# Opening each gate graph with the product S1 T1, and issuing the sums for the next graph one beat sooner

## The chip, the cores and the metric

The kernel runs on one core of one Trainium2 chip. The metric is the time of one execution on the device, in microseconds (us). Beside it stands a profiled execution, whose trace gives the start and the length of every instruction on each engine: TensorE (PE, with its weight loads listed apart as PEld), VectorE (DVE), ScalarE (ACT), GpSimd (POOL), and the DMA queue that SyncE issues (SP).

## The reference, cut to what matters

There are 64 graphs with 256 nodes and 256 features each. Layer 0 is a graph convolution; its result is x2, and h2 is x2 after a layer norm and a relu. Layer 1 works on h2. A convolution with 17 taps along the nodes gives x_conv, message passing gives x_nmp, and a gated unit mixes them:

```python
x_in = jnp.concatenate([x_conv, x_nmp], axis=-1)
gi = x_in @ w_ih.T + b_ih
gh = x @ w_hh.T + b_hh              # x is h2 here
r = jax.nn.sigmoid(gi_r + gh_r)
z = jax.nn.sigmoid(gi_z + gh_z)
nn_ = jnp.tanh(gi_n + r * gh_n)
return (1.0 - z) * nn_ + z * x      # and then x2 is added
```

All numbers are 32-bit floats.

## The kernel before, in words

**Two stages.** The first stage, up to about 885 us, computes layer 0, the messages and the first part of the convolution, and starts the spectral convolution of graphs 0 to 15. The second stage computes the gates. It has four parts of 16 graphs. Part q computes the gates of 16 graphs and, in the first three parts, the spectral convolution of the next 16: first their spectra, then 24 products by frequency (`product`), three ahead of the gates and six inside each graph until they are used up, which is in the fourth graph. The inverse transform of these products runs on VectorE and GpSimd through the rest of the part. At its end `turn_outputs` transposes the outputs into the tile `xcT`, which the next part reads.

**One graph of gates** is `gates(ld, between, nxt)`. The r and z gates for two halves of 128 nodes would need four sums of six 128-row products. They are computed as seven (Strassen's scheme): each call of `three` is three accumulated matmuls, each of which has two records in the trace. Its inputs are plain tiles (`hx` from memory, `xcT`), sums of them called S1 to S4, and sums of weights called T1 to T4. The order on TensorE, with a name that the text uses for each:

- P1 into `ta` columns RC, P2 into `tb` RC, P3 into `tb` ZC, P5 = S1 T1 into `tc` ZC;
- `between[0]()`, a convolution product where there is one;
- P6 = S2 T2 onto `ta`, P7 = S4 W2 onto `tc`, the six matmuls of the n gate for the first half (`gates_n(ld, 0)`), P4 = S3 T3 onto `ta`;
- the rest of `between`, and `gates_n(ld, 1)`.

P1 and P5 accumulate onto a bias that ScalarE has copied into the bank ahead (`bank_of`). For the next graph the copy into `tc` is made in `first_rows`, behind the tanh of the first half, and the copy into `ta` in `second_rows`, one beat later. `tb` is claimed anew by each graph.

**Beats.** After each group of matmuls stands a `beat(us)`. `after(k, go)` puts off a piece of work for another engine to the (k+1)-th beat from there. A beat issues what has come due, in the order of registration, and then a share of the paced work of the inverse transform (`Paced`), as far as the room that the beat adds allows: a two-operand VectorE operation costs 0.5 for 256 elements and 0.85 for 512. All engines keep the program's order, so the place of an issue is the place in its engine's queue.

**The sums.** `gate_parts` returns two functions: `s12` (three VectorE operations: two adds that make S1, one subtraction that makes S2) and `s34` (three GpSimd operations that make S4 and S3). S1 and S2 have two buffers each, S3 and S4 one. For the first graph of a part they are called directly; for the others `gates` of the graph before registers them as `nxt`. A beat is counted here from the graph's start in a graph without products: beat 1 follows P1, and beats 7, 8 and 9 follow the n matmuls of the first half, P4, and the n matmuls of the second half.

Of the kernel before, what the change touches and what calls it, by code (L numbers as in the profile page):

```python
# [82 lines left out]
def add(e, o, a, b):  # L83
    e.tensor_tensor(o, a, b, ALU.add)
# [101 lines left out]
def gnn_kernel(  # L186
# [60 lines left out]
    def after(beats, go):  # L247
        due.append([beats, go])

    def come_due():  # L250
        now = []
        for d in list(due):
            d[0] -= 1
            if d[0] < 0:
                now.append(d[1])
                due.remove(d)
        for go in now:
            go()
# [286 lines left out]
    with ExitStack() as one:  # L545
# [11 lines left out]
        def beat(us):  # L557
            come_due()
            paced.issue(*(k * us for k in share))
# [93 lines left out]
        def taps_part(hold, oc, cc, k0):  # L653
            n = min(4, KW - k0)
            t = bank(f"t_w2_{oc}_{cc}_{k0}")
            for k in range(n):
                pe.transpose(
                    t[:, k * P : (k + 1) * P],
                    hold[oc][:, cc * P : (cc + 1) * P, k0 + k],
                    ident,  # L660
                )

            def keep():
                evict(
                    w2T[cc][:, k0 : k0 + n, oc * P : (oc + 1) * P],
                    t[:, : n * P].rearrange("p (k o) -> p k o", k=n),
                )
                if oc == DC - 1:
                    nc.sync.dma_start(
                        wt_d[k0 : k0 + n, cc * P : (cc + 1) * P].rearrange("k c o -> c k o"),  # L670
                        w2T[cc][:, k0 : k0 + n],
                    )
            after(0, keep)
            beat(0.4)
# [77 lines left out]
        def gate_turn(tag, dst, o0, i):  # L752
# [8 lines left out]
        parts = [  # L761
            [lambda oc=oc, cc=cc, k0=k0: taps_part(hold, oc, cc, k0)
             for cc in range(DC) for k0 in range(0, KW, 4)]
            for oc in range(DC)
        ]
# [532 lines left out]
    def outputs_turned(q):  # L1298
# [16 lines left out]
    RC, ZC = slice(0, D), slice(D, 2 * D)  # L1315
    W1 = [whT[:, 0], whT[:, 1], wiT[:, DC]]
    W2 = [wiT[:, 0], wiT[:, 1], wiT[:, DC + 1]]
    T1, T2, T3, T4 = (
        big.tile([P, 3, D], FP, tag=f"T{k}", name=f"T{k}") for k in range(1, 5)
    )  # L1320
# [17 lines left out]
    def gate_rows(ld):  # L1338
        n, q, g = ld["n"], ld["q"], ld["g"]
        ld["h2"] = h2 = io2.tile([P, NB, D], FP, tag="h2l", name=f"h2l_{n}")  # L1340
        nc.sync.dma_start(
            h2, h2_d[q][g * N : (g + 1) * N].rearrange("(c p) d -> p c d", p=P)
        )
        ld["x2"] = x2 = io2.tile([P, NB, D], FP, tag="x2l", name=f"x2l_{n}")
        nc.sync.dma_start(x2, x2_d[n].rearrange("(c p) d -> p c d", p=P))
# [31 lines left out]
    def three(dst, A, W, start):  # L1377
        for k in range(3):
            pe.matmul(
                dst, A[k], W[k], start=(start and k == 0), stop=(k == 2), skip_group_check=True  # L1380
            )

    def parts(S):
        return [S[:, k] for k in range(3)]

    def copied(ld, src, tag):
        ld[tag] = t = sm2.tile([P, D], FP, tag=tag, name=f"{tag}_{ld['n']}", bufs=1)
        act.copy(t, src)
# [3 lines left out]
    def bank_of(tag):  # L1392

        k = banks.get(tag, 0)
        banks[tag] = k + 1
        t = ps_gate.tile([P, 2 * D], FP, tag=tag, name=f"{tag}_{k}", bufs=1 + (tag == "n"))
        if tag == "n":
            act.copy(t, bnB)
        elif tag == "ta":
            act.copy(t[:, RC], brzB[:, RC])  # L1400
        else:
            act.copy(t[:, ZC], brzB[:, ZC])
        return t
# [3 lines left out]
    def gates_n(ld, nb):  # L1407

        pn = ready.pop(("n", nb))
        for off, pairs in (  # L1410
            (D, list(zip(ld["A1"][nb][:DC], (whT[:, c] for c in range(DC))))),
            (0, [(ld["A1"][nb][DC], wiT[:, DC])]
             + list(zip(ld["A2"][nb], (wiT[:, 0], wiT[:, 1], wiT[:, DC + 1])))),
        ):
            for k, (a, w) in enumerate(pairs):
                pe.matmul(
                    pn[:, off : off + D], a, w[:, 2 * D :],
                    start=False, stop=(k == len(pairs) - 1), skip_group_check=True,
                )
        ld[f"pn{nb}"] = pn  # L1420

    def gates_out(ld, nb):

        n, h2, x2, pn, rz = ld["n"], ld["h2"], ld["x2"], ld[f"pn{nb}"], ld["rz"][nb]
        uu = sm2.tile([P, D], FP, tag="u", name=f"u_{n}_{nb}")
        nn = sm2.tile([P, D], FP, tag="nn", name=f"nn_{n}_{nb}")
        df, ot = h2[:, nb, :], x2[:, nb, :]


        def inner():  # L1430
            vec.scalar_tensor_tensor(uu, rz[:, RC], 1.0, pn[:, D:], ALU.add, ALU.mult)
            vec.scalar_tensor_tensor(uu, uu, 0.5, pn[:, 0:D], ALU.mult, ALU.add)

        def outer():
            act.activation(nn, uu, AF.Tanh)
            ready["n", nb] = bank_of("n")


        def plain():
            e = vec if n == B - 1 and nb == NB - 1 else pool  # L1440
            e.tensor_tensor(df, df, nn, ALU.subtract)
            e.tensor_tensor(ot, ot, nn, ALU.add)

        def scaled():
            vec.scalar_tensor_tensor(df, rz[:, ZC], 1.0, df, ALU.add, ALU.mult)
            vec.scalar_tensor_tensor(ot, df, 0.5, ot, ALU.mult, ALU.add)
            dst = out[n].rearrange("(c p) d -> p c d", p=P)
            if n == B - 1:
                nc.sync.dma_start(dst[:, nb], ot)
            elif nb == NB - 1:  # L1450
                nc.sync.dma_start(dst, x2)

        after(2, inner)
        after(3, outer)
        after(4, plain)
        after(5 if n == B - 1 else 6, scaled)

    def gates(ld, between, nxt):


        n = ld["n"]
        ta, tc_ = ready.pop("ta"), ready.pop("tc")
        tb = ps_gate.tile([P, 2 * D], FP, tag="tb", name=f"tb_{n}", bufs=1)
        rz = [
            sm2.tile([P, 2 * D], FP, tag=f"rz{k}", name=f"rz_{n}_{k}", bufs=1) for k in range(NB)
        ]
        ld["rz"] = rz
        three(ta[:, RC], ld["A1"][0], [w[:, RC] for w in W1], False)
        after(1, lambda: copied(ld, ta[:, RC], "p1"))
        beat(1.3)  # L1470
        three(tb[:, RC], ld["A2"][0], [w[:, RC] for w in W2], True)
        after(2, lambda: add(vec, rz[0][:, RC], ld["p1"], tb[:, RC]))
        beat(1.3)
        three(tb[:, ZC], ld["A2"][1], parts(T4), True)
        beat(1.3)
        three(tc_[:, ZC], parts(ld["S1"]), parts(T1), False)
        after(1, lambda: copied(ld, tc_[:, ZC], "p5"))
        beat(1.3)
        between[0]()
        three(ta[:, RC], parts(ld["S2"]), parts(T2), False)  # L1480
        after(1, lambda: copied(ld, ta[:, RC], "u2"))
        beat(1.3)
        three(tc_[:, ZC], parts(ld["S4"]), [w[:, ZC] for w in W2], False)

        def first_rows():
            act.activation(rz[0], rz[0], AF.Tanh, scale=0.5)
            ready["tc"] = bank_of("tc")
        after(1, lambda: add(vec, rz[0][:, ZC], ld["u2"], tc_[:, ZC]))
        after(2, first_rows)
        beat(1.3)  # L1490
        gate_rows(ld)
        gates_n(ld, 0)
        gates_out(ld, 0)
        beat(2.6, v=0.2)
        three(ta[:, RC], parts(ld["S3"]), parts(T3), False)

        def second_rows():
            copied(ld, ta[:, RC], "u3")
            ready["ta"] = bank_of("ta")
            add(vec, rz[1][:, RC], ld["u3"], tb[:, ZC])  # L1500
        after(1, second_rows)
        after(2, lambda: add(pool, rz[1][:, ZC], ld["u3"], ld["p5"]))
        after(3, lambda: act.activation(rz[1], rz[1], AF.Tanh, scale=0.5))
        beat(1.3, v=0.4)
        for go in between[1:]:
            go()
        gates_n(ld, 1)
        gates_out(ld, 1)
        if nxt is not None:
            after(0, nxt[0])  # L1510
            after(1, nxt[1])
        beat(2.6, v=0.8, g=0.7)


# [10 lines left out]
    for q in range(1, GROUPS + 1):  # L1525
        share[:] = 0.6, 0.6, 0.3
        ld = gate_inputs(q - 1, 0)
# [19 lines left out]
        for g in range(NG):  # L1547
            share[:] = (0.42, 0.55, 0.3) if todo else (0.51, 0.62, 0.3)
            between = [todo.pop(0) if todo else lambda: None for _ in range(PER)]
            ahead, nxt = None, None  # L1550
            if g + 1 < NG:
                ahead = gate_inputs(q - 1, g + 1)
                nxt = gate_parts(ahead, xcT)
            gates(ld, between, nxt)
            ld = ahead
# [36 lines left out]
```

## Time and profile before

| what | value |
|---|---|
| median of 3 runs (lowest, highest) | 2079.03 us (2078.04, 2083.53) |
| profiled execution, its own time | 2078.45 us |
| its span, first to last instruction | 2076.7 us |
| TensorE busy | 2028.5 us, 98% of the span |
| its weight loads busy | 1727.0 us, 83% |
| VectorE busy | 1404.7 us, 68% |
| ScalarE busy | 997.5 us, 48% |
| GpSimd busy | 1108.9 us, 53% |
| mean granted TensorE clock | 0.997 |

A row of the profile gives the engine, the operation, the tiles that it writes and reads (written<-read), their shapes, and behind a bar the busy time and the mean of one; "idle before" is the time in which the engine had nothing to run ahead of it, with the engine and tile whose end released it. Since a helper records all operations, they carry the same line number, L102; the tiles tell them apart. In the timeline `rz<-u,tc` is VectorE's sum for the first half's z gate, `S<-hx,xcT` and `S<-hx` are the two adds of S1, `S<-S,hx` makes S2, `Xf` and `scr` are the inverse transform, `y` the banks of the convolution products.

### The profile page before, as it was taken

To read this page: it belongs to the slowest core of one execution; us is meant where nothing else is said; L and a number is where in the kernel's file an instruction comes from. 1 tells how busy PE (TensorE), PEld (TensorE's weight loads), DVE (VectorE), ACT (ScalarE), POOL (GpSimd) and SP (SyncE) were. 2 spreads that over 40 slices of the span, in tenths; PEclk is the share of its full clock that TensorE was granted. 3 is DMA by queue.
4 is the path that set the end of the run, shared out by engine and by line. 5 is a ranking of instruction groups with operands and counts; after the bars stand their busy time and mean duration, and the time that the engine had idled before them with its cause. 6 is when DMAs were issued, how large, how long until landed. Compare 5 with 4: busy or idle time off the path is not lost. (4 is left out here: it accounts for less than half of the span.)

```text
span 2076.7 us, 31189 instructions
## 1 busy us (share of the span) xinstructions
PE 2028.5 (98%) x9977; PEld 1727.0 (83%) x9977; DVE 1404.7 (68%) x3181; ACT 997.5 (48%) x2165; POOL 1108.9 (53%) x1313
## 2 busy tenths in 40 slices
PE   7999999999999999899999999999999999999998
PEld 6877777888888787788888888888888888888887
DVE  6656666544688887337889815989924989965444
ACT  5756666665457676522344532234442234443333
POOL 4343333334775665347667527766726767644433
PEclk9999999999999999999999999999999999999999
DMA  9697987657765554656333455533346424322231
GB/s 307 241 255 245 264 252 251 208 178 228 242 203 195 178 178 148 202 178 203 122 117 117 138 177 187 167 102 117 126 154 195 155 92 127 117 87 89 95 97 61
DMA packets 292456, 352.84 MB, mean 170 GB/s; under 512 B 19491, under 2 KB 232118, under 8 KB 291638
## 3 DMA queue, kind: packets, MB, share of 16 engines
q1 hardware_dynamic: 291680, 346.26, 52.5%
q0 software_dynamic: 288, 4.46, 0.6%
q8 instruction: 80, 1.31, 0.3%
q14 instruction: 82, 0.67, 0.1%
q10 hardware_dynamic: 326, 0.14, 0.0%
HBM read 224.43 MB, written 126.35 MB: 169 GB/s over the span
## 5 line engine op out<-in xcount | busy, mean ns | idle before, releaser
L102 DVE SCALAR_TENSOR_TENSOR Xf<-Xf 128x256 f32<-128x256 f32 (+1 forms) x248 | 185.7, 763 | 6.1 <-ACT Xf L102 5.1
L102 DVE TENSOR_TENSOR Xf<-y,k 128x256 f32<-128x256 f32 x184 | 69.0, 416 | 178.3 <-PE y L102 175.3
L102 PE MATMUL ta<-T,S 128*128 128x256 f32 x768 | 186.6, 379 | 0.0
L102 PE MATMUL y<-wf,Xf 128*128 128x256 f32 x768 | 182.4, 380 | 2.5 <-DVE Xf L102 1.4
L102 POOL TENSOR_TENSOR rz<-u,p 128x256 f32<-128x256 f32 x64 | 48.0, 749 | 244.6 <-ACT u L102 244.6
L102 POOL TENSOR_TENSOR rs<-ve,mhalf 128x2 f32<-128x2 f32 (+1 forms) x65 | 52.2, 803 | 226.8 <-DVE nm L102 221.6
L102 ACT ACTIVATE rz<-rz 128x512 f32<-128x512 f32 x128 | 80.2, 627 | 180.6 <-DVE rz L102 180.6
L102 PEld LDWEIGHTS y<-wf,Xf 128*128 128x128 f32 x768 | 144.0, 190 | 24.9 <-DVE Xf L102 2.6
L102 PEld LDWEIGHTS ta<-T,S 128*128 128x128 f32 x768 | 145.9, 190 | 19.8
L102 PE MATMUL n<-wiT,hx 128*128 128x256 f32 x512 | 152.3, 379 | 0.0
L102 POOL TENSOR_TENSOR xs<-Xf 128x256 f32<-128x256 f32 x92 | 69.9, 766 | 133.9 <-PE y L102 72.7
L102 DVE SCALAR_TENSOR_TENSOR h2l<-rz,h2l 128x256 f32<-128x256 f32 x128 | 102.8, 803 | 53.6 <-POOL h2l L102 53.6
L102 POOL TENSOR_TENSOR aT<-e,adjT 128x512 f32<-128x512 f32 x64 | 85.8, 1358 | 94.1 <-ACT e L102 94.1
L102 PE MATMUL n<-whT,hx 128*128 128x256 f32 x512 | 131.4, 379 | 0.0
L102 PE MATMUL n<-wiT,xcT 128*128 128x256 f32 x512 | 131.4, 379 | 0.0
L102 PE MATMUL o<-w0T,aggT 128*128 128x256 f32 x512 | 125.6, 388 | 5.7 <-ACT aggT L102 4.1
L102 PE MATMUL ag<-adjH,hs 128*128 128x256 f32 x512 | 123.0, 382 | 7.5 <-POOL adjH L102 6.1
L102 PE MATMUL nm<-aT,mso 128*128 128x256 f32 x512 | 123.0, 384 | 7.1 <-POOL aT L102 4.5
L102 PE MATMUL ms<-wmT,h2T 128*128 128x259 f32 x512 | 124.3, 385 | 1.5 <-DVE h2T L102 1.5
L102 POOL TENSOR_TENSOR adjH<-adjT,eye 128x512 f32<-128x512 f32 x64 | 83.6, 1306 | 76.8 <-ACT adjT L102 76.8
L102 PE MATMUL c<-w1T,h2T 128*128 128x256 f32 x512 | 122.8, 383 | 0.0
L102 PEld LDWEIGHTS o<-w0T,aggT 128*128 128x128 f32 x512 | 95.3, 191 | 28.7 <-issue 5.6
(183 smaller groups left out, 5253.1 us busy)
## 6 DMA issues: line engine op xcount, KB each, us to landing
wf<-wfd SPq DMA_DIRECT2D x284, 256.0 KB
wfd<-fo SPq DMA_DIRECT2D x32, 576.0 KB
x2d<-x SPq DMA_DIRECT2D x64, 256.0 KB
h2d<-h SPq DMA_DIRECT2D x64, 256.0 KB
hTd<-h2T SPq DMA_DIRECT2D x64, 256.0 KB
h1d<-c1o SPq DMA_DIRECT2D x64, 256.0 KB
xnd<-xnT SPq DMA_DIRECT2D x64, 256.0 KB
h1l<-h1d SPq DMA_DIRECT2D x64, 256.0 KB
```

The source lines that it names most:

```text
L102: return self.tc.keep_in_program_order(getattr(self.engine, op)(*args, **kwargs))
```

## The change

The call of `three` for P5, with the put-off copy of its result (`p5`) and a beat, moves from the fourth place to the first. P1, P2 and P3 follow it, one place later each. The registration of `nxt` moves from after `gates_n(ld, 1)` to ahead of the beat that follows P4, and the second of its functions is registered for two beats after its first possible one, not one.

```diff
         ld["rz"] = rz
+        three(tc_[:, ZC], parts(ld["S1"]), parts(T1), False)
+        after(1, lambda: copied(ld, tc_[:, ZC], "p5"))
+        beat(1.3)
         three(ta[:, RC], ld["A1"][0], [w[:, RC] for w in W1], False)
         after(1, lambda: copied(ld, ta[:, RC], "p1"))
         beat(1.3)
...
         three(tb[:, ZC], ld["A2"][1], parts(T4), True)
-        beat(1.3)
-        three(tc_[:, ZC], parts(ld["S1"]), parts(T1), False)
-        after(1, lambda: copied(ld, tc_[:, ZC], "p5"))
         beat(1.3)
         between[0]()
...
         after(3, lambda: act.activation(rz[1], rz[1], AF.Tanh, scale=0.5))
+        if nxt is not None:
+            after(0, nxt[0])
+            after(2, nxt[1])
         beat(1.3, v=0.4)
         for go in between[1:]:
             go()
         gates_n(ld, 1)
         gates_out(ld, 1)
-        if nxt is not None:
-            after(0, nxt[0])
-            after(1, nxt[1])
         beat(2.6, v=0.8, g=0.7)
```

So `s12` is issued at beat 8 in place of beat 9. In a graph without products `s34` is issued at beat 1 of the next graph as before; in a graph with products, where up to ten more beats lie between P4 and `gates_n(ld, 1)`, both come that much earlier.

## The prediction

> **What bounds the kernel now.** I read the page first, then the waits of TensorE in the gate stage, then the windows of three graphs, then timelines where a wait ended. The page:
>
> ```profile
> span 2076.7 us, 31189 instructions
> PE 2028.5 (98%) x9977; PEld 1727.0 (83%) x9977; DVE 1404.7 (68%) x3181; ACT 997.5 (48%) x2165; POOL 1108.9 (53%) x1313
> ```
>
> TensorE is busy all the time. A busy PE can still be stretched, so I took start to start: in the gates it is 216 ns per record wherever no wait shows. A graph without products has 66 records, 14.26 us, and the third of the windows below lasts 14.25. There is nothing to win in such a graph; the change can only take away, or make, waits of TensorE. Those from 885 us on, longest first, as total, times and longest:
>
> ```profile
> PE ta L102 <- ACT ta L102: 3.3, 3, 1.1
> PE yt L102 <- ACT xcT L102: 1.8, 6, 0.3
> PE y L102 <- DVE Xf L102: 1.4, 3, 0.5
> ```
>
> Three graphs as windows (starting at 1058.81, 1130.40 and 1942.07):
>
> ```profile
> 1058.81:1073.31 14.50, 14.41 (x67) 12.35 (x65) 12.08 (x23) 4.92 (x13) 10.55 (x12) 1.00 0.36 113
> 1130.40:1145.91 15.51, 14.41 (x68) 12.35 (x66) 14.42 (x23) 4.87 (x13) 12.83 (x14) 1.00 0.36 115
> 1942.07:1956.32 14.25, 14.25 (x68) 12.54 (x67) 6.92 (x14) 5.00 (x12) 5.92 (x8) 1.00 0.27 93
> ```
>
> The columns are length, then busy time of PE, PEld, DVE, ACT, POOL. Only the first line of waits is what the change aims at: P1 waiting for the bias in `ta`. Start to start it is 0.26 us more than 216 ns at the start of graph 9 (1073 us), 1.27 at graph 14 (1145 us), and 0.10 more on the next record each time. Graphs 25, 30, 41 and 46 repeat this. Together 3 x (0.36 + 1.37) = **5.2 us, 0.25%: the most that can be won at these waits.** Where they are, VectorE is full (14.42 of 15.51 us). At graph 14:
>
> ```profile
> 1144.21 0.59 PE L102 MATMUL n<-wiT,hx 128*128 128x256 f32 x2
> 1145.91 1.13 PE L102 MATMUL ta<-whT,hx 128*128 128x256 f32 x4 [1.10 <-ACT ta L102]
> ```
>
> ScalarE's own timeline there, and VectorE's:
>
> ```profile
> 1144.24 0.63 ACT L102 ACTIVATE rz<-rz 128x512 f32<-128x512 f32 x1 [6.80 <-DVE rz L102]
> 1144.78 0.37 ACT L102 COPY tc<-brzB 128x256 f32<-128x256 f32 x1
> ...
> 1145.48 0.38 ACT L102 COPY ta<-brzB 128x256 f32<-128x256 f32 x1
> ```
>
> ```profile
> 1143.80 0.41 DVE L102 TENSOR_TENSOR rz<-u,tc 128x256 f32<-128x256 f32 x1
> 1144.13 0.41 DVE L102 SCALAR_TENSOR_TENSOR Xf<-scr 128x256 f32<-128x256 f32 x1
> 1144.58 0.76 DVE L102 SCALAR_TENSOR_TENSOR scr<-Xf 128x256 f32<-128x256 f32 x2
> 1145.26 0.41 DVE L102 SCALAR_TENSOR_TENSOR u<-rz,n 128x256 f32<-128x256 f32 x1
> ...
> 1146.38 0.42 DVE L102 TENSOR_TENSOR S<-hx,xcT 128x256 f32<-128x256 f32 x1
> 1146.71 0.28 DVE L102 TENSOR_TENSOR S<-hx 128x128 f32<-128x128 f32 x1
> ```
>
> TensorE could go on at 1144.64 (its last record is half of the first row's two). The cause is VectorE, whose `rz<-u,tc` is late; ScalarE's tanh, the copy to `tc` and the copy to `ta` follow it in order.
>
> **What the Trainium skill says.** "Perfetto Trace Analysis", section Identifying the Most-Contended Engine: matmul busy time does not tell how near TensorE is to its peak, and weight-load occupancy is a better sign. Here they are 98% and 83%; the 216 ns spacing says the same, so I count waits, not busy time. "SBUF — State Buffer", section Who interferes with whom: a VectorE operation with two SBUF inputs contends with a GpSimd operation that reads SBUF. The trace agrees: `S<-hx,xcT` takes 412 ns at the least, 426 in the median, 809 at the most.
>
> **The change, part by part.** No matmul, copy, sum or DMA is added or removed; one call of 6 records (6 x 0.216 = 1.3 us) changes places with 18.
>
> *P1 three places of slack to the good.* The copy to `ta` may end 1.3 us later than before. At graph 14 it ends at 1145.86, and P1 could begin at 1144.64 + 1.30 = 1145.94. The old waits vanish: -5.2 us.
>
> *P5 in the first place needs `tc` and S1.* `tc` is filled 0.7 us before `ta` (ends 1145.15), and still 0.5 us after 1144.64. S1 is issued at beat 8, ahead of that beat's paced work. Following the pacing rule through graph 13, two paced operations of 256 go at beat 7 and one at beat 8, so S1 starts behind `rz<-u,tc` and two of the three paced ones, near 1144.93. The first add takes 0.42; the second ends 0.61 after the start of the first. I can't tell whether P5's first matmuls wait for one or for both, so S1 is there at 1145.35 or 1145.54, and 0.05 us goes to the signal (the `ta` copy ends at 1145.86, the matmul starts at 1145.91). The new wait is 0.76 to 0.95, plus the 0.10. The same reckoning for graph 9 (both paced ones at beat 7, S1 starts 1072.60, free at 1073.05) gives 0 to 0.20 plus 0.10, and for graph 11 (1101.32, free at 1101.91) 0 to 0.07 plus 0.10, where there was no wait. Next come graph 12 with 0.4 us in hand and graph 8 with 0.9; all others have over 1.4. Per part 0.86 to 1.52 in place of 1.73; over three parts **-2.6 to -0.6 us net** with the line above.
>
> *The first graph of the last part (48)* has no products and no spectra ahead of it. P1 reads only `hx` and covered the last copies into `xcT`:
>
> ```profile
> 1842.35 1.03 PE L102 MATMUL ta<-whT,hx 128*128 128x256 f32 x4
> 1842.56 0.75 DVE L102 TENSOR_SCALAR xcT<-yt,sh 128x512 f32<-128x512 f32 x1 [0.53 <-PE yt L102]
> ...
> 1843.40 0.42 DVE L102 TENSOR_TENSOR S<-hx,xcT 128x256 f32<-128x256 f32 x1
> 1843.74 0.28 DVE L102 TENSOR_TENSOR S<-hx 128x128 f32<-128x128 f32 x1
> ```
>
> P5 must wait until 1843.87 or 1844.07 in place of 1842.35: **+1.5 to +1.8 us**, with nothing after it to pay it back, since TensorE is full to the end.
>
> *The sums in graphs with products.* In the third graph of a part s12 (1.1 us of VectorE at its pitch) and s34 (0.8 + 0.5 + 1.0 us of GpSimd) now lie among the products, where the wait `y <- Xf` of the list falls (0.62 us at 971 us; 1300 and 1629 too). VectorE has 0.86 + 0.17 us idle between 964 and 966.4 to swallow s12; GpSimd's `h2l` goes back behind s34 and holds VectorE's scaled sum by some tenths. I take +0.3 us each, between 0 and 1.0: **+0.9 (0 to 3)**. The earlier graphs of a part have no paced VectorE work there, and the fourth has no product left whose bank could be late.
>
> *Costed at nothing.* `hx` for the next graph is issued 0.24 us after a graph's start, and s12's new place is 8 us or more after it, even in graph 12 where SP issues late (1105.0 against 1113.9); SP's order doesn't change, and nothing of s12 is moved past its issues. If a load took longer than 8 us, s12 would hold VectorE and all queued behind it. The `p5` copy moves from beat 5 to beat 2, ahead of `p1`; the tanh that waits for GpSimd already stands in front of it. P1's copy has 2.6 us until P6 in place of 3.9; ScalarE takes 0.4. `rz[0]` RC moves to beat 5 and is needed at beat 8. s12 ahead of `u<-rz,n` and `rz<-u,tb` sets them back by up to 1.3 us, and P2 needs `tb` free, but P2 begins 1.3 us later as well; its margin was 0.67 us at the least and stays.
>
> *Sum:* (-2.6 to -0.6) + (1.5 to 1.8) + 0.9 = -0.2 to +2.1; the middle is +1.0 us. Against the profiled execution's 2078.45 us that is **2079.5 us**; the median of the three runs, 2079.03, is 0.6 above that execution.
>
> **Rivals.** *The waits go altogether (0.20).* If VectorE, relieved at beat 9, comes to `rz<-u,tc` half a microsecond sooner and P5 waits for the first add alone, little is left at graphs 9 and 14: -5.2 + 1.5 = -3.7, 2074.8 us. For it speaks that P5 asks for the bank that is filled first; against it that the three operations only change places on a full VectorE, all ahead of the same `rz<-u,tc`. *S1 becomes the bound (0.15).* S1 had 3.9 us from its graph's start; now it has none. Where GpSimd contends, the adds take up to 0.8 us each in place of 0.42 and 0.28, and a delay of 1 us at graphs 9, 11, 12 and 14 would add some 1.5 us per part (a wait of TensorE lets VectorE catch up, so they don't add in full), with s34 at the upper end of its cost: +1.0 + 4.5 + 2.1, 2086 us. It decides from about 0.7 us of delay; against it speaks that GpSimd is idle at graph 14 until 1145.5. *It doesn't do what it says* can't be excluded in one sense: the bank `tc` alone, without S1, already keeps 0.5 us of graph 14's wait; that lies inside my sum.
>
> **Numbers.** 0.65 for the forecast, with its own range 2077.5 to 2082; 0.20 and 0.15 for the rivals. The range of 8 in 10 is 2075.5 to 2085. What can be told from no change is about 0.3%, 6.2 us: 2072.8 to 2085.3. The first rival doesn't reach the lower bound, since all that the waits hold is 5.2 us; 0.05 remains for what no row shows. Of the second a half lies beyond the upper one. So faster 0.05, same 0.88, slower 0.07.
>
> **What would show it.** Right: no wait `ta <- ACT ta`; in its place `tc` waiting for DVE `S` at graphs 14, 30 and 46, about 0.9 us start to start; one wait of 1.5 to 1.8 us at graph 48; graphs of the last part still 14.25 us; the wait at `y` in the third graph of a part a little longer. Wrong: waits of TensorE from 885 us on that fall or rise by over 4 us in all, or a plain graph that isn't 14.25 us.

## The result, and the profile after

| kernel | median | lowest, highest | runs | against the kernel before, 95% interval |
|---|---|---|---|---|
| before | 2079.12 us | 2077.86, 2083.53 | 6 | |
| changed | 2087.03 us | 2086.01, 2088.70 | 6 | 1.0037 (1.0026 to 1.0047) |

The change costs 7.9 us, 0.37%. The forecast was 2079.5 us with a range to 2085, so the time lies outside it, on the slow side.

The profiled execution took 2088.70 us. Its page:

```profile
span 2086.9 us, 31130 instructions
PE 2031.1 (97%) x9977; PEld 1727.0 (83%) x9977; DVE 1402.2 (67%) x3181; ACT 992.8 (48%) x2165; POOL 1102.0 (53%) x1313
```

The span is 10.2 us longer. The second stage is counted here from its first matmul, which fills its banks, at 844.8 us before and 847.9 us changed; the first turning of outputs and the first spectra lie between that and 885 us. What stands ahead of it, which the change doesn't touch, took between 843.7 and 847.9 us in the profiles of all the runs below, and 3.1 us of the 10.2 lie there. The second stage went from 1231.9 to 1239.0 us. These 7.2 us are to be explained. The waits of TensorE from 885 us on, as total, times and longest:

```profile
PE ta L102 <- ACT p L102: 7.6, 6, 1.8
PE y L102 <- DVE Xf L102: 2.1, 3, 0.7
PE yt L102 <- ACT xcT L102: 1.8, 6, 0.3
PE tc L102 <- DVE S L102: 1.4, 1, 1.4
```

The line `ta <- ACT ta` is gone, as forecast. A longer line stands in its place, which the forecast doesn't have: `ta <- ACT p`, twice in each of the first three parts. Taken start to start, with the slower record behind a wait, the second stage adds up so:

| wait | before | changed | difference |
|---|---|---|---|
| P1 for its bank `ta` | 5.2 | 0 | -5.2 |
| P6 for the copy `p<-ta` | 0 | 9.2 | +9.2 |
| P5 of graph 48 for S1 | 0 | 1.6 | +1.6 |
| products for their bank `y` | 5.5 | 6.6 | +1.1 |
| spectra `df`, most of it for a load | 3.3 | 3.7 | +0.4 |
| sum | | | +7.1 of 7.2 |

The larger of the new waits comes ahead of P6 of graph 11 (and 27, 43). TensorE and then ScalarE there, in the changed kernel:

```profile
1110.31 0.59 PE L102 MATMUL tb<-T,hx 128*128 128x256 f32 x2
1112.69 1.56 PE L102 MATMUL ta<-T,S 128*128 128x256 f32 x6 [1.79 <-ACT p L102]
```

```profile
1111.44 0.42 ACT L102 ACTIVATE nn<-u 128x256 f32<-128x256 f32 x1 [2.40 <-DVE u L102]
1111.76 0.58 ACT L102 COPY n<-bnB 128x512 f32<-128x512 f32 x1
1112.28 0.37 ACT L102 COPY p<-ta 128x256 f32<-128x256 f32 x1
```

P1 was done at about 1108.3, and P6 adds onto `ta`, so it must wait for the copy of P1's result. That copy takes 0.37 us but starts at 1112.28: in ScalarE's queue it stands behind `nn`, ahead of which ScalarE stood idle for 2.40 us until VectorE had made `u`. In the kernel before, the same place of ScalarE's timeline is

```profile
1103.58 0.35 ACT L102 COPY p<-ta 128x256 f32<-128x256 f32 x1
1106.64 0.42 ACT L102 ACTIVATE nn<-u 128x256 f32<-128x256 f32 x1 [2.71 <-DVE u L102]
```

Here `p<-ta` stands ahead of `nn`. `nn` of the graph before falls due at beat 3. P1's copy fell due at beat 2; one place later, it falls due at beat 3 too, and `nn` was registered first. This `nn` is that of the second half of graph 10, and so is the `u` that it reads. VectorE's timelines of the changed kernel, and then of the kernel before, show why `u` is late:

```profile
1104.35 0.41 DVE L102 TENSOR_TENSOR S<-hx,xcT 128x256 f32<-128x256 f32 x1
1104.68 0.81 DVE L102 TENSOR_TENSOR S<-hx 128x128 f32<-128x128 f32 x1
1105.53 0.97 DVE L102 TENSOR_TENSOR S<-S,hx 128x384 f32<-128x384 f32 x1
...
1107.99 2.63 DVE L102 SCALAR_TENSOR_TENSOR Xf<-Xf 128x256 f32<-128x256 f32 x2
1110.54 0.41 DVE L102 SCALAR_TENSOR_TENSOR u<-rz,n 128x256 f32<-128x256 f32 x1
```

```profile
1102.43 0.81 DVE L102 TENSOR_TENSOR S<-hx,xcT 128x256 f32<-128x256 f32 x1
1103.16 0.28 DVE L102 TENSOR_TENSOR S<-hx 128x128 f32<-128x128 f32 x1
1103.47 0.56 DVE L102 TENSOR_TENSOR S<-S,hx 128x384 f32<-128x384 f32 x1
...
1104.29 1.54 DVE L102 SCALAR_TENSOR_TENSOR Xf<-Xf 128x256 f32<-128x256 f32 x2
1105.75 0.41 DVE L102 SCALAR_TENSOR_TENSOR u<-rz,n 128x256 f32<-128x256 f32 x1
```

VectorE works without a pause in both. In the changed kernel the three sums take 2.07 us (1104.35 to 1106.42, where the next operation starts), where the forecast reckoned 1.1; before they took 1.52. The new place of the sums isn't what delays this `u`: from `rz<-u,tc` of graph 10 to it, the same twelve operations run in both kernels, with the sums ahead of the first half's `u` in one and behind it in the other. They take 8.48 us in place of 6.72, because they are longer: the sums by 0.55 us, the pair of `Xf<-Xf` by 1.09. Counted from the start of graph 11, `u` starts at 4.98 us in place of 3.84. An estimate from these rows: with `u` as early as before, the new order on ScalarE alone would have made P6 wait 0.8 of its 1.95 us here. The windows of graphs 4 to 15 of the first part, before and then changed (length, then PE, PEld, DVE, ACT, POOL busy):

```profile
1001.83:1174.50 172.67, 171.47 (x793) 150.27 (x792) 158.32 (x285) 69.37 (x172) 117.11 (x127) 1.00 0.35 112
```

```profile
1005.84:1179.85 174.01, 171.47 (x793) 150.27 (x792) 162.26 (x287) 67.90 (x172) 114.36 (x125) 1.00 0.36 113
```

The stretch is 1.34 us longer (4.0 us over three parts, the 9.2 less the 5.2), TensorE's busy time is the same, and VectorE's has grown by 3.9 us with two operations more. From 885 us on, none of the 63 subtractions `S<-S,hx` overlapped a GpSimd operation in the kernel before; 12 of 63 do in the changed one.

### The profile page after: what moved, and what is told of

It is laid out like the page before. It is cut to its first block, busy times and chain, and to the rows that moved or that the text cites. A ratio compares the mean times of both kernels' runs of the same rounds, so it can differ in the third digit from the quotient of the medians.

```text
span 2086.9 us, 31130 instructions
## 1 busy us (share of the span) xinstructions
PE 2031.1 (97%) x9977; PEld 1727.0 (83%) x9977; DVE 1402.2 (67%) x3181; ACT 992.8 (48%) x2165; POOL 1102.0 (53%) x1313
## 5 line engine op out<-in xcount | busy, mean ns | idle before, releaser
L102 ACT COPY u<-ta 128x256 f32<-128x256 f32 x128 | 47.6, 372 | 279.1 <-PE ta L102 279.1
L102 ACT COPY k<-y 128x512 f32<-128x512 f32 x92 | 53.9, 585 | 159.3 <-PE y L102 158.3
L102 POOL TENSOR_TENSOR h2l<-h2l,nn 128x256 f32<-128x256 f32 x127 | 109.5, 862 | 29.0 <-ACT nn L102 28.1
```

What stands on the lines that cost most here:

```text
L102: return self.tc.keep_in_program_order(getattr(self.engine, op)(*args, **kwargs))
```

## The experiments

Two theories on the 7 us. **S**: each wait of TensorE stands by itself, and the copy's place in ScalarE's queue makes the one at P6 (theory Q in the first four runs). **V**: VectorE is late in graphs 4 to 15 of a part, and its lateness comes out wherever TensorE needs something behind it (theory D, in the first four runs, is its first form: the sums at beat 8 cause the delay, whatever ScalarE's order).

| run | median | ratio to before, interval | second stage of the profile |
|---|---|---|---|
| before | 2078.75 to 2079.86 in the sets of runs below | | 1231.9 |
| changed | 2087.03 | 1.0037 (1.0026 to 1.0047) | 1239.0 |
| e1 copy one beat sooner | 2084.24 | 1.0025 (1.0016 to 1.0033) | 1237.7 |
| e2 order alone | 2092.06 | 1.0062 (1.0050 to 1.0075) | 1244.5 |
| e3 sums alone | 2083.96 | 1.0020 (1.0013 to 1.0028) | 1236.2 |
| e4 `nn` one beat later | 2085.08 | 1.0029 (1.0019 to 1.0039) | 1238.4 |
| e5 before, bank ahead of tanh | 2095.30 | 1.0071 (1.0058 to 1.0083) | 1246.1 |
| e6 changed, no S2 | 2078.88 | 0.9998 (0.9990 to 1.0007) | 1234.5 |
| e7 mended | 2080.99 | 1.0009 (1.0001 to 1.0018) | 1234.0 |
| e9 before, no S2 | 2075.70 | 0.9982 (0.9974 to 0.9991) | 1228.7 |
| e10 before, S2 on GpSimd | 2086.97 | 1.0041 (1.0028 to 1.0053) | 1238.3 |
| e11 changed, S2 on GpSimd | 2091.58 | 1.0059 (1.0046 to 1.0073) | 1243.1 |
| e12 mended, S2 on GpSimd | 2082.36 | 1.0015 (1.0008 to 1.0021) | 1233.2 |
| e13 before, paced work earlier | 2084.00 | 1.0027 (1.0015 to 1.0038) | 1240.5 |

Sizes of waits below are start to start over the second stage, unless a profile line is shown.

**e1: P1's copy one beat sooner**, ahead of `nn`.

```diff
-        after(1, lambda: copied(ld, ta[:, RC], "p1"))
+        after(0, lambda: copied(ld, ta[:, RC], "p1"))
```

> The changed kernel with the ScalarE copy of P1's result put off by after(0) in place of after(1): it is issued at the beat right behind P1, ahead of the tanh nn and the bank copy n of the graph before. Theory Q (the copy p<-ta stands in ScalarE's queue behind nn, which waits for VectorE, and P6 waits for it): the wait of ta on ACT p vanishes (9.2 us start to start, 7.6 by the waits), and the time falls to about 2078, at or just under the kernel before. Rival D (VectorE's sums at beat 8 are what delays the chain, whatever the order on ScalarE): P6 or P7 waits for another ScalarE result in its place and the time stays within 2 us of 2087.

Its waits of TensorE from 885 us on:

```profile
PE tc L102 <- ACT u L102: 3.4, 3, 1.1
PE yt L102 <- DVE xcT L102: 3.2, 9, 0.5
PE df L102 <- DMA h1l<-h1d: 2.5, 5, 1.0
```

The wait for `p` is gone, so the place in ScalarE's queue did make it. But of the 9.2 us only 2.8 came back in the median. At graph 14 P5 now waits (3.9 us over the three parts). The row names ScalarE's copy into `u`, which P5 doesn't read and which ended at 1146.82, just ahead of P5's start at 1146.86. Of what P5 reads, `tc` was filled by 1146.52 and S1's first add ended at 1146.72, so the likelier cause is S1. The turned outputs `yt` wait 1.7 us more than before, and the spectra 2.0 us more for a load than in the changed kernel. The time is in neither theory's band; Q has the wait right and the gain wrong.

**e2: P5 first, sums at beat 9 as before.**

> P5 first as in the changed kernel, but the sums registered at beat 9 as in the kernel before. Theory Q: the copy p<-ta still stands behind nn, but nn's input on VectorE comes earlier by the 1.1 us of s12, so the wait of ta on ACT p is about halved or less (0 to 4 us); P5 now waits for S1 in the graphs where VectorE is full, 1 to 5 us per part; in all 2083 to 2092. Rival D: with the sums back at beat 9 no wait on ACT p is left at all, and only P5's waits for S1 remain.

```profile
PE tc L102 <- DVE S L102: 13.0, 10, 1.8
```

No wait for `p` is left, as rival D says and as the lower end of Q's range allows; P5 waits for S1 instead, three times per part and once at graph 48, and the time is the upper end of Q's band. The run doesn't decide between the two: P5's wait stops TensorE shortly ahead of P6, which gives ScalarE and VectorE time to catch up. It does show that P5 can't go first without waits while the sums stay where they were.

**e3: the sums at beat 8, order of the products as before.**

> The kernel before with the sums registered ahead of the beat after P4 and nothing else changed. Theory Q: the copy p<-ta is issued at beat 2, ahead of nn, so there is no wait of ta on ACT p; P1's wait for its bank stays (5.2 us), the wait at y in the third graph of a part grows by about 0.6 us as in the changed kernel; 2079 to 2081. Rival D: the sums ahead of u<-rz,n cost the better part of the 8 us by themselves, 2084 to 2087.

```profile
PE tb L102 <- DVE rz L102: 3.6, 6, 0.7
...
PE ta L102 <- ACT ta L102: 1.1, 3, 0.4
```

The time is the lower edge of rival D's band, with a wait that neither theory named: P2 for the bank `tb`, which VectorE's `rz<-u,tb` frees, and that operation now stands behind the sums. P1's wait fell from 5.2 to 1.9, P2's is 5.2. The sums one beat sooner cost 4 us by themselves.

**e4: `nn` and the bank copy `n` behind P1's copy**, with the copy where the change put it.

```diff
-        after(3, outer)
+        after(4, outer)
```

> The changed kernel with the step that issues nn and the bank copy n one beat later (after(4) in place of after(3)), so that it stands behind the copy p<-ta; the copy's own place is that of the changed kernel. Theory Q: the wait of ta on ACT p vanishes here too, 2077 to 2080, unless the later nn makes GpSimd's h2l and x2l late. Rival D: no change, 2085 to 2089.

```profile
PE yt L102 <- ACT xcT L102: 3.8, 3, 1.3
PE yt L102 <- DVE xcT L102: 3.6, 9, 0.4
```

The wait for `p` is gone again, as Q says, but the time lies in rival D's band. Graphs 4 to 15 are faster than in the kernel before (515.7 us over the three parts against 518.0). But the time moved to the end of the part: turning the outputs takes 32.3 us against 28.2. How much of that comes from the later `nn` itself was not separated. In e1 and e4 a wait was taken away and others stand elsewhere, which is what V says. The next four runs were made to tell V from S.

**e5: the kernel before, with P1's bank ahead of the late tanh.**

```diff
-        after(2, first_rows)
+        after(3, first_rows)
...
-        after(1, second_rows)
+        after(0, second_rows)
```

> The kernel before, with ScalarE's order at P4 turned round: the copies u3 and ta (second_rows, and VectorE's add behind it) are issued one beat sooner, at beat 8, and the tanh of the first half with the copy into tc (first_rows) one beat later, at beat 9. P1's bank no longer stands behind a tanh that waits for VectorE. Theory S (each wait of TensorE stands by itself): P1's 5.2 us vanish and nothing comes in their place, 2074 to 2075.5. Theory V (VectorE is late in graphs 4 to 15 of a part and its delay has to be paid somewhere before the outputs are turned): P1's waits vanish, but waits at tb, at P7 or at yt take over half of it or more, 2076 to 2080.

Both missed by far. P1's waits are gone; these came, all from VectorE or behind it:

```profile
PE yt L102 <- DVE xcT L102: 6.1, 9, 1.4
PE y L102 <- DVE Xf L102: 5.5, 3, 1.8
PE tb L102 <- DVE rz L102: 3.3, 6, 0.9
PE tc L102 <- ACT p L102: 2.7, 6, 0.6
```

VectorE's add `rz<-u,tb` was issued a beat sooner as well, and waits there for ScalarE's `u`, with all of VectorE's queue behind it. VectorE's own waits in the first part (885 to 1190 us), before and then e5:

```profile
DVE rz L102 <- ACT u L102: 3.1, 5, 0.8
```

```profile
DVE rz L102 <- ACT u L102: 13.0, 7, 3.8
```

Ten microseconds more of this wait of VectorE in the first part stand beside some five more of TensorE's time per part (14.2 us over the three).

**e6 and e9: VectorE relieved.** S2's subtraction is left out and S1 used in its place, in the changed kernel and in the kernel before.

```diff
+        S2 = S1
...
-            sub(vec, S2, S1, hx[:, 0:3, tok[0]])
```

> The changed kernel with VectorE relieved: the subtraction that makes S2 is left out and S1 is used in its place (so the gates are not those of the reference), which takes one operation of about 0.5 to 0.7 us per graph off VectorE and changes no order. Theory V: ScalarE's nn, which waits for VectorE, comes earlier with each graph, and the wait of ta on ACT p falls from 9.2 us start to start to under 2; about 2078 to 2080. Theory S (the copy's place on ScalarE alone): the wait stays over 6 us; 2084 to 2087. The wait at graph 48 stays at 1.5 to 1.6 us with both.

> The kernel before with the same operation left out as in the run e6 (S1 in place of S2; the gates are not those of the reference). Theory V: P1's waits for ta, which follow VectorE's late sum, fall from 5.2 us to under 1, and nothing takes over: 2074 to 2076. Theory S has the same waits at graphs 9 and 14 at over half of their size: 2076 to 2079. The difference between e6 and this run is what the change costs when VectorE isn't late: 1.6 us at graph 48 and 0 to 1.5 at y.

Waits in e6, the longest first, and what is left of P1's in e9:

```profile
PE df L102 <- DMA h1l<-h1d: 3.7, 3, 2.7
PE y L102 <- DVE Xf L102: 2.1, 3, 0.7
PE yt L102 <- ACT xcT L102: 1.8, 6, 0.3
PE tc L102 <- DVE S L102: 1.4, 1, 1.4
```

```profile
PE ta L102 <- ACT ta L102: 0.5, 3, 0.2
```

V holds in both, though P1's 1.3 us are a little above its "under 1". With one operation in 24 fewer per graph, no order changed, the wait for `p` falls from 9.2 to 0.7 us, P1's in the kernel before from 5.2 to 1.3, and nothing takes over: graphs 4 to 15 come down to 513.5 and 514.1 us, against 36 x 14.25 = 513.0 for graphs without any wait. What the change costs when VectorE isn't late is the rest: 1.6 us at graph 48 and 1.6 at `y`; the medians differ by 3.2. (The second stages of the two profiles differ by more, 5.8 us, of which 3.2 lie at the spectra: in e6 one of them waited 2.7 us for a load, and TensorE then ran at half its clock for 3.4 us; see the last section.) Leaving S2 out also lets GpSimd start S4 sooner, so the two runs relieve VectorE first and GpSimd with it.

**e7: the changed kernel with three repairs**: P1's copy as in e1, P1 first at graph 48 alone, sums at the old place in graphs with products.

```diff
+        late = n == (GROUPS - 1) * NG
+        if not late:
+            product_5()
         three(ta[:, RC], ld["A1"][0], [w[:, RC] for w in W1], False)
-        after(1, lambda: copied(ld, ta[:, RC], "p1"))
+        after(0, lambda: copied(ld, ta[:, RC], "p1"))
...
-        if nxt is not None:
+        if nxt is not None and not products:
             after(0, nxt[0])
             after(2, nxt[1])
```

> The changed kernel with three repairs: the copy of P1's result is issued one beat sooner (as in the run e1); the first graph of the last part keeps the order of before, P1 first and P5 fourth; and in graphs with products the sums are registered where they were before. Theory S: against the run e1 (2084.2) the wait of 1.6 us at graph 48 goes and the waits at y fall back by 0.5 to 1.5 us: 2081 to 2082. Theory V: the same at graph 48, but the sums back among the last beat of the product graphs leave VectorE with more to do in graph 4, and the gain at y is given back at tc or yt: 2082 to 2083.5.

```profile
PE tc L102 <- ACT u L102: 3.3, 3, 1.1
PE yt L102 <- DVE xcT L102: 3.1, 9, 0.4
```

2080.99 is a hair below S's band. The wait at graph 48 is gone and `y` is back at 5.3. What remains over the kernel before, 1.9 us, is in the profile P5's wait at graph 14 (4.2 us over the parts), 1.7 more at `yt` and 1.1 more at the spectra, less P1's 5.2.

**e10, e11, e12: S2 on GpSimd**, which is busy 68% of graphs 4 to 15, in the kernel before, the changed kernel and e7.

```diff
-            sub(vec, S2, S1, hx[:, 0:3, tok[0]])
...
         def s34():
+            sub(pool, S2, S1, hx[:, 0:3, tok[0]])
```

> The kernel before with S2's subtraction on GpSimd, at the head of the sums that GpSimd makes (S4 and S3), in place of VectorE. The outputs are the reference's. Theory V: VectorE is relieved as in the run e9 (2075.7), P1's waits for ta fall from 5.2 us start to start to under 1; GpSimd takes on about 1 us per graph and may make P7 wait for S4 or VectorE for h2l: 2075 to 2078. Rival: GpSimd, 68% busy in graphs 4 to 15 of a part, becomes late itself and its h2l and Xf hold VectorE: 2079 to 2084.

> The changed kernel with S2's subtraction on GpSimd in the same way. Theory V: the wait of ta on ACT p goes as in the run e6 (2078.9), 1.5 us at graph 48 stay, 2078 to 2081. Rival: as for e10, 2082 to 2087.

> The run e7 with S2's subtraction on GpSimd: P5 first, P1's copy one beat sooner, graph 48 and the product graphs as before. Theory V: the waits of tc (3.8 us) and yt that e7 kept go as well, 2075 to 2078, level with e10 or just under it. Rival: as for e10, 2079 to 2084.

V's times are wrong in all three. The rival has the sign right, but its sizes are too small in two: e10 is 3.0 us above its band and e11 4.6 above; e12 lies in it. In e10 VectorE is busy 16 us less in the three stretches and GpSimd 35 us more, and P1's waits still rise from 5.2 to about 9.7 us. VectorE's longest wait in graphs 4 to 15 of the first part, before and then e10:

```profile
DVE h2l L102 <- POOL h2l L102: 7.7, 7, 1.8
```

```profile
DVE h2l L102 <- POOL h2l L102: 15.5, 10, 3.1
```

In e11 the wait for `p` falls from 9.2 to 3.3 us, but the products' waits for `y` rise from 6.6 to 12.6; the line of the list was 2.1 in the changed kernel:

```profile
PE y L102 <- DVE Xf L102: 7.9, 9, 1.6
```

A wider V fits these runs: VectorE and GpSimd hand results back and forth, and it is the pair that is late, so that work moved from one to the other doesn't relieve it. That is argued, not shown by itself. No run relieved GpSimd alone, and the move also made the subtraction longer (1.11 us in the median on GpSimd in e10, 0.56 on VectorE before) and later by one beat.

**e13: the kernel before, more of the paced work in graphs with products.**

```diff
-            share[:] = (0.42, 0.55, 0.3) if todo else (0.51, 0.62, 0.3)
+            share[:] = (0.55, 0.55, 0.3) if todo else (0.51, 0.62, 0.3)
```

> The kernel before with a larger share of VectorE for the paced inverse transform in graphs that still have products (0.55 in place of 0.42), where VectorE is busy 61% of the time; the order of the gates is that of before, no operation is added. Theory V: paced work goes over from the full graphs 4 to 15 of a part to graphs 2 and 3, P1's waits for ta fall from 5.2 us start to start to under 2, the waits at y in graphs 2 and 3 grow by up to 2; 2075 to 2079. Rival (VectorE's work there is tied to GpSimd's, so that what is issued sooner only waits for GpSimd's results in VectorE's queue): P1's waits stay or the waits at y take over, 2079 to 2083.

```profile
PE y L102 <- DVE Xf L102: 5.6, 3, 1.9
PE y L102 <- DMA wf<-wfd: 1.9, 2, 1.1
```

P1's waits fall to 1.7 us, as V says, but `y` goes from 5.5 to 15.6 us: the rival's mechanism, a little above its band. Not all of that is waiting. Behind the longest wait TensorE's records start 0.43 us apart in place of 0.216 for 3.4 us, and the trace has a granted clock of 0.50 there (the third number from the end):

```profile
976.64 2.64 PE L102 MATMUL y<-wf,Xf 128*128 128x256 f32 x8 [1.86 <-DVE Xf L102]
```

```profile
977.85:981.25 3.40, 3.40 (x10) 2.68 (x9) 2.83 (x9) 0.59 (x1) 0.18 (x1) 0.50 0.49 139
```

It happens in each of the three parts and takes 1.7 us each time, 5.0 of the 10.1 us. The profiled execution, 2088.54 us, was the slowest of the seven; how often it happened in the others isn't known.

No kernel with the reference's arithmetic was faster than the kernel before.

## Why the prediction was wrong, point by point

- *Only waits of TensorE matter; 216 ns per record; a graph without products 14.25 us.* Right: the changes of the waits add up to 7.1 of the 7.2 us.
- *P1's waits for its bank vanish, -5.2 us.* Right.
- *Costed at nothing: "P1's copy has 2.6 us until P6 in place of 3.9; ScalarE takes 0.4."* **This is the step that failed.** I compared the copy's own length with the slack, and asked for the `p5` copy what stands ahead of it, but not for P1's. Being one place later it changed sides with `nn`, which waits for VectorE. P6 waited 9.2 us for it, where the forecast had nothing; e1 and e4, which turn that order back in two ways, have no such wait. In the time e1 won 2.8 us and e4 2.0, since other waits took its place.
- *"s12 ahead of `u<-rz,n` and `rz<-u,tb` sets them back by up to 1.3 us"*, with no one waiting but P2. At graph 11 the sums set the first half's `u` back by 2.1 us. The second half's `u`, which P6 waits for through `nn`, stands behind the sums in both kernels; it is late because VectorE's operations there took 1.76 us longer. P2 kept its margin in the changed kernel, since P2 moved as well; e3, where it didn't move, shows the wait at once.
- *P5's new waits at graphs 9, 11 and 14, 0.9 to 1.5 us per part.* None came. At graph 14 the likely reason is P6's wait at graph 11, which let VectorE catch up: where it is taken away (e1), a wait at graph 14 comes with 1.3 us, inside the range for a part. At graphs 9 and 11, which P6's waits don't precede, none came in either kernel.
- *Graph 48, +1.5 to +1.8 us.* Right: 1.52 start to start and 0.10 on the next record. P5 starts 0.05 us after the end of the first add, which settles what I had left open:

```profile
1852.47 0.48 PE L102 MATMUL tc<-T,S 128*128 128x256 f32 x1 [1.36 <-DVE S L102]
```

```profile
1851.99 0.43 DVE L102 TENSOR_TENSOR S<-hx,xcT 128x256 f32<-128x256 f32 x1
1852.34 0.28 DVE L102 TENSOR_TENSOR S<-hx 128x128 f32<-128x128 f32 x1
```

- *Sums among the products, +0.9 (0 to 3).* +1.1.
- *The second rival* had the right sign, place (graphs of a full VectorE) and size, 2086 us, but the wrong wait: P5 never waited for S1 there. That its size agrees is luck.
- What I didn't ask is what the waits have in common. The kernel before paid VectorE's and GpSimd's lateness at P1, and I treated each wait as a loss of its own. e6 and e9, where P1's and P6's waits both go with one VectorE operation, show that they were one debt. With the order of before, the sums at beat 8 cost 4 us (e3), mostly at P2's bank, where the order does it. At graph 11 of the changed kernel it is the longer operations; for the other graphs the two were not separated.

## What to carry to other kernels

When a producer moves by one place, look at each engine that reads its result and list what now stands ahead of that reader in the queue, and what that waits for; the reader's own length says nothing. Before a wait is chased away, find which engine is late behind it: if that engine has no slack over the stretch, the wait can come out at the next point of contact. In these runs only less work on VectorE made the whole faster than the kernel before. A test for this is cheap: leave one operation of the suspected engine out, though the result is then wrong, and see whether all the waits go.

## What the runs showed of the hardware

- A VectorE add of 128x128 with two inputs in on-chip memory took 0.28 us alone and 0.81 beside GpSimd's work, and the subtraction of 128x384 0.56 and 0.97 (graph 48 and graph 11 of the changed kernel). Over the changed kernel from 885 us on, the subtraction took 0.56 us in the 51 graphs where no GpSimd operation overlapped it, and 0.56 to 1.09 in the 12 where one did. The Trainium skill, "SBUF — State Buffer", section Who interferes with whom, says that a VectorE operation with two SBUF inputs contends with a GpSimd operation that reads SBUF; these traces agree, and the durations are theirs.
- After a wait the next record of TensorE came 0.10 us later than its spacing of 216 ns, in each of the waits at P1 and P6; it comes on top of the wait.
- Behind some waits of TensorE the traces have a granted clock of 0.50 for 3.4 us, which cost about 1.7 us each time: after 1.86 us of idle time in each part of e13, after 2.49 in the first part of e10, after 2.69 in e6. It did not follow the same wait of e10 in the other two parts, nor the 1.79 us at P6 in the changed kernel. What decides it isn't shown.
